# Three-part products added in one bank, attention by groups of four heads, and an order written out for three engines

## The chip, the cores and the metric

The kernel runs on one core of a Trainium2 chip. The metric is the device time of one execution in microseconds; less is better. The inputs are 64 batches of 256 rows by 512 columns, all in fp32, and the outputs are held to the fp32 reference.

## The reference, cut to what matters

```python
def gnn0(x, adj, Wq, bq, Wk, bk, Wv, bv, Wo, bo):     # 8 heads of 64
    q = (x @ Wq + bq).reshape(b, n, H, HD)             # k, v likewise
    scores = einsum('bqhd,bkhd->bhqk', q, k) / sqrt(HD)
    scores = scores + (1.0 - adj)[None, None] * -1e9
    out = einsum('bhqk,bkhd->bqhd', softmax(scores), v).reshape(b, n, d)
    return out @ Wo + bo

x = layernorm(x + gnn0(x, adj, ...))
y = einsum('nm,bmd->bnd', adj, x)
x = layernorm(x + einsum('bnd,do->bno', y, weight) + bias)
```

adj is 256 by 256 of zeros and ones, one eighth of them ones. There are five products with a 512 by 512 weight for each batch: q, k, v, o (the output of attention) and l (the second layer).

## The kernel before, in words

Two batches make a pair; there are NP = 32 pairs. `fast` does them all; `general` runs only where values leave the range that `fast` can treat (a small count at the end decides it), and it does not run here.

**Products in parts.** A large product is not done in whole fp32. Both operands are split into three fp32r parts (high, low, diff), and `part_product` (L318, its matmul is L321) multiplies part by part. A product is cut into four blocks j; a block is one PSUM bank of 128 by 512. `near` does parts 1 (low) and 0 (high) into the bank, then ACT multiplies the bank in place by 1 + 1/4096 (L333), and `far`, later, adds part 2 (diff) and takes the bank out: to R for o and l (L345, with the row sums for the norm), to V (L354), or to Q and K (L359). The two calls are held apart by a list, LAGGED, so that PE has other blocks between them. The split is `cut_low` (L168 masks bits off, L169 subtracts) and `difference` (L174) on DVE, and a rounding copy to high on ACT (L282 for x, L305 for o and l). Weights are split once (`split_w`), written to DRAM, and read again as parts for each pair through a ring of six 1 MB tiles (`load_w`, L127, on POOL's queue). Only v, q and k of the first two pairs take the weights as whole fp32.

**Attention.** A unit is four heads of one batch; a pair has four units. `scores` (L374) fills four banks, ACT takes the exponential (L378), DVE multiplies by the mask (L384) and adds the two halves of the keys (L390). `values` sums the exponentials with ones (L402, copied out at L404), multiplies by V (L410, copied at L413), and `divided` transposes, inverts and multiplies on DVE (L420 to L426).

**Norms and the second layer.** `norm` takes the mean from the row sums, ACT squares (L452), POOL takes the power -0.5 (L457), ACT applies scale and offset (L484). `halves` splits the result in two parts (L506 on ACT, L507 on DVE), `adj_x` multiplies by adj (L520) and ACT copies the bank to Y (L522), which `chunk_parts` then splits for l. `biased` (L436) adds a bias to R ahead of a product.

**Order.** A window w has scores and values of pair w, o and l of pair w - 1, v, q and k of pair w + 1, and x of pair w + 2. `between` writes the steps as a list, with four slots in which the values of the last unit and the scores of the next stand. Steps that follow on others are put off by a count of ticks (`later`). The list is the order of PE, ACT and DVE in windows 1 to 30; in window -1 of PE and DVE, in window 0 and in the last window of PE alone. Where an engine is not named, the framework's planner orders its instructions; SP's and POOL's queues are always its.

**Buffers.** PSUM has four banks for attention (`ps_at`) and four for the rest (`ps_mm`). A buffer is given out again when its last reader is done.

Of the kernel before, what the change touches and what calls it, by code (L numbers as in the profile page):

```python
# [19 lines left out]
FINE = 4096.0  # L32
MASKED = -1000000000.0
# [10 lines left out]
def fast(tc, x, adj, wq, bq, wk, bk, wv, bv, wo, bo, w1, b1, out):  # L44

    nc = tc.nc
# [6 lines left out]
    assert B % 2 == 0 and B > 2 and D == 512 and N == 256 and HD == 64  # L53
    qscale = 1.0 / math.sqrt(HD)

# [9 lines left out]
    xpool = pool("xp", 1)  # L65
    stage = pool("stage", 4)
    parts = pool("parts", 4)
    chunks = pool("chunks", 3)
    differences = pool("differences", 4)
    wring = pool("wr", 6)  # L70
    scratch = pool("scratch", 1, space=bass.MemoryType.DRAM)
    rpool = pool("rp", 2)
    one = pool("one", 1)
    qk = pool("qk", 3)
    four = pool("four", 4)
    small = pool("small", 2)
    ps_at = pool("ps_at", 4, space=bass.MemoryType.PSUM)
    ps_mm = pool("ps_mm", 4, space=bass.MemoryType.PSUM)

    XC, R, XF, XG, XL, XD, Q, K, V, E, SM, O, HL, Y, ST, CP, CUT = ({} for _ in range(17))  # L80

    def load_x(p, i):

        if p < NP:
            t = XC[p, i] = stage.tile([P, D], F32, name="x")
            for q in range(4):
                nc.sync.dma_start(t[q * 32:(q + 1) * 32].rearrange("i (m j) -> i m j", j=32), xb[p, i, q])

    def load_r(p):
        if p < NP:  # L90
            t = rpool.tile([P, 2, NC, D], F32, name="r")
            nc.sync.dma_start(t, xr[p])
            R[p] = [t[:, b] for b in range(2)]

    ones = cpool.tile([P, 32], F32, name="ones")
    nc.gpsimd.memset(ones, 1.0)
    for i in range(4):
        t = XC[0, i] = four.tile([P, D], F32, name="v")
        nc.sync.dma_start(t, xc[0, i // 2, i % 2])
    ident = one.tile([P, P], F32, name="zc")  # L100
    make_identity(nc, ident)
# [6 lines left out]
    def on_all(b, name):  # L108
# [5 lines left out]
    SOURCE = dict(v=wv, q=wq, k=wk, o=wo, l=w1)  # L114
    WP, SCRATCH, RAW = {}, {}, {}


    STREAM = [(name, p, i) for w in range(1, NP - 1) for name, p in
              (("o", w - 1), ("v", w + 1), ("q", w + 1), ("k", w + 1),
               *([("l", w - 1)] if w < NP - 2 else [("o", w), ("l", w - 1)])) for i in range(3)]  # L120

    def load_w(n=1):
        for _ in range(n):
            if STREAM:
                name, p, i = STREAM.pop(0)
                t = wring.tile([P, DC, D], F32R, name="wr")
                nc.gpsimd.dma_start(t, SCRATCH[name, i])  # L127
                WP[name, p, i] = t

    def raw_weight(name, tiles, queue):  # L130

        for i in range(3):
            SCRATCH[name, i] = scratch.tile([P, DC, D], F32, name=f"{name}{i}")
        n = DC // len(tiles)
        for i, t in enumerate(tiles):
            for k in range(n):
                RAW[name, i * n + k] = t[:, k]
            w = SOURCE[name][i * n * P:(i + 1) * n * P]
            if name == "o":


                for a in range(n):
                    queue.dma_start(t[:, a], w.rearrange("(h a i) e -> a h i e", h=4, a=2)[a])
            else:
                queue.dma_start(t, w.rearrange("(c p) e -> p c e", p=P))

    def split_w(name, k):

        high, low, diff = (parts.tile([P, D], F32R, name=n) for n in ("high", "low", "diff"))
        cut = one.tile([P, D], F32, name="cut")  # L150
        cut_low(RAW[name, k], cut, low)
        difference(RAW[name, k], low, diff)
        nc.scalar.activation(high, cut, AF.Copy)
        nc.scalar.activation(low, low.bitcast(F32), AF.Copy, scale=FINE)
        nc.scalar.activation(diff, diff.bitcast(F32), AF.Copy, scale=-1 / FINE)
        for i, part in enumerate((high, low, diff)):
            nc.sync.dma_start(SCRATCH[name, i][:, k], part.bitcast(F32))


    LOADS = [(1 + n // 4, n % 4) for n in range(4 * NP - 4)]  # L160

    def load_next():
        if LOADS:
            load_x(*LOADS.pop(0))

    def cut_low(a, cut, low):

        nc.vector.tensor_scalar(cut.bitcast(I32), a.bitcast(I32), -int(FINE), None, op0=OP.bitwise_and)  # L168
        nc.vector.tensor_tensor(low, a, cut, op=OP.subtract)  # L169

    def difference(a, low, diff):


        nc.vector.scalar_tensor_tensor(diff, low.bitcast(F32), -(FINE + 1), a, op0=OP.mult, op1=OP.add)  # L174

    raw_weight("v", [four.tile([P, 2, D], F32, name="o") for _ in range(2)], nc.scalar)

    nc.scalar.activation(small.tile([P, 1], F32, name="table"), ones[:, 0:1], AF.Exp)
    whole = lambda: [rpool.tile([P, DC, D], F32, name="r")]
    raw_weight("q", whole(), nc.sync)  # L180
    bq_s, bk_s = by_partition(bq, "bq"), by_partition(bk, "bk")
    raw_weight("k", whole(), nc.sync)
    adj_s = one.tile([P, NC, N], F32, name="sm")
    nc.sync.dma_start(adj_s, adj.rearrange("(c p) m -> p c m", p=P))
    for _ in range(4):
        load_next()
# [3 lines left out]
    bo_s, b1_s = on_all(bo, "bo"), on_all(b1, "b1")  # L190

    power = cpool.tile([P, 4], F32, name="power")
# [3 lines left out]
    acc = cpool.tile([P, N // 32], F32, name="acc")  # L196

    def adj_t():
# [6 lines left out]
        square = one.tile([P, NC, N], F32, name="vc")  # L205
# [3 lines left out]
        nc.vector.tensor_reduce(acc[:, 0:1], square, AX.XY, OP.max)  # L209
        nc.vector.tensor_scalar(acc, acc, RANGE * RANGE, None, op0=OP.mult)  # L210

    def bv_wo():

        wide = one.tile([P, DC, P], F32, name="vc")
        nc.vector.tensor_copy(wide, bv_s[:, :, None].to_broadcast([P, DC, P]))
        pm = ps_mm.tile([P, D], F32, name="mm")
        for d in range(DC):
            nc.tensor.matmul(pm, wide[:, d, :], RAW["o", d], start=d == 0, stop=d == DC - 1)
        nc.vector.tensor_tensor(bo_s, bo_s, pm, op=OP.add)
# [3 lines left out]
    due = []  # L223

    def later(n, f, *args):
        due.append([n, f, args])

    def tick():
        for d in due:
            d[0] -= 1  # L230
        ready = [d for d in due if d[0] <= 0]
        due[:] = [d for d in due if d[0] > 0]
        for _, f, args in ready:
            f(*args)

    BANKS = {}


    DEEP = [("l", NP - 3, 1), ("l", NP - 3, 3)] + [(n, p, j) for n in "ol" for p in (NP - 2, NP - 1) for j in (1, 3)]
    DEEP.remove(("o", NP - 2, 1))  # L240

    def x_t(p, i):
        xs = XC.pop((p, i))
        if p == 0:
            pt = ps_mm.tile([P, DC, P], F32, name="mm")
            if i == 0:
                for d in range(DC):
                    if d % 2 == 0:  # L250
                        t = qk.tile([P, 2, D], F32, name="kT")
                    XF[p, d] = t[:, d % 2]
            for d in range(DC):
                nc.tensor.transpose(pt[:, d, :], xs[:, d * P:(d + 1) * P], ident)
            for d in range(DC):
                to = XF[p, d][:, i * P:(i + 1) * P]
                if d % 2:
                    nc.scalar.activation(to, pt[:, d], AF.Copy)
                else:
                    nc.vector.tensor_copy(to, pt[:, d])  # L260
        else:
            if p > 1:
                XF[p, i] = xpool.tile([P, D], F32, name="xT")
                XC[p, i] = xs
            elif i % 2 == 0:
                t = four.tile([P, 2, D], F32, name="o")
                XF[p, i], XF[p, i + 1] = t[:, 0], t[:, 1]
            nc.vector.transpose(XF[p, i], xs)  # L268
            if p == 1:
                load_next()  # L270

    def x_parts(p, k):
        XG[p, k], XL[p, k] = (parts.tile([P, D], F32R, name=n) for n in ("high", "low"))
        cut_low(XF[p, k], XC[p, k], XL[p, k])
        later(1, x_high, p, k)

    def x_diff(p, k):
        XD[p, k] = parts.tile([P, D], F32R, name="diff")
        difference(XF.pop((p, k)), XL[p, k], XD[p, k])

    def x_high(p, k):
        nc.scalar.activation(XG[p, k], XC.pop((p, k)), AF.Copy)  # L282
        load_next()

    def chunk_parts(name, p, j):

        a = (O if name == "o" else Y)[p, j // 2][:, j % 2].rearrange("p k i -> p (k i)")  # L290
        cut = one.tile([P, D], F32, name="cut")
        if (name, p, j) in DEEP:
            high, low, diff = (parts.tile([P, D], F32R, name=n) for n in ("high", "low", "diff"))
        else:
            high, low = (chunks.tile([P, D], F32R, name=n) for n in ("chigh", "clow"))
            diff = differences.tile([P, D], F32R, name="cdiff")
# [27 lines left out]
    def near(name, p, j):  # L324
# [4 lines left out]
        if (name, p, 1) in WP:  # L329
            part_product(pm, name, p, j, 1)  # L330
# [510 lines left out]
```

## Time and profile before

| | us |
|---|---|
| median of 3 runs | 2533.59 (2533.59 to 2536.14) |
| span of the profiled execution, first to last instruction | 2536.9 |
| the profiled execution's own time | not listed apart from the span, which is 3.3 above the median |
| busy PE / DVE / ACT / POOL | 2492.1 / 1870.3 / 1709.9 / 386.1 |
| mean granted TensorE clock | 0.994 of full |
| moved by DMA | 600.25 MB, 237 GB/s in the mean |

A busy time is the union of an engine's instructions in the trace. Matmuls overlap, so PE's pace is read from the distances between starts in the timeline, not from its busy time or from a matmul's mean. In a line of the costliest groups come the source line, engine and operation, out<-in by the program's names, the shape and count, busy time and mean ns of one, and then the idle time ahead of them with what ended it.

### The profile page before, as it was taken

What the parts mean: (1) busy time and instruction counts of PE and PEld (TensorE: products, weight loads), DVE (VectorE), ACT (ScalarE), POOL (GpSimd) and SP (SyncE); (2) the same over time, 40 slices, a digit from 0 to 9 for tenths busy, and PEclk for the clock granted to TensorE, in tenths of its full rate; (3) what the DMA queues carried; (4) which work ended last, traced back from release to release, by engine and by line L of the source; (5) the groups of instructions that cost most, each with busy time, mean ns of one, the idle gap of its engine ahead of it and who ended that gap; (6) DMA issues with size and microseconds to landing.
All of it is one profiled execution on the core that took longest, in us unless ns stands there. A gap on an engine that the chain in (4) does not pass through costs nothing.

```text
span 2536.9 us, 42179 instructions
## 1 busy us (share of the span) xinstructions
PE 2492.1 (98%) x15806; PEld 1895.2 (75%) x15806; DVE 1870.3 (74%) x3239; ACT 1709.9 (67%) x3206; POOL 386.1 (15%) x793
## 2 busy tenths in 40 slices
PE   8999999999999999999999999999999999999997
PEld 4477777777777777777777777777777777777765
DVE  4577887777877768877768876778877778777687
ACT  4556666776666776667776667766667766667755
POOL 0111111111111111111111111111111111111111
PEclk9999999999999999999999999999999999999998
DMA  7777778687787787787787777877777877777721
GB/s 205 268 219 243 245 252 249 237 268 223 236 259 256 230 281 225 233 261 246 240 262 240 245 247 247 254 245 240 252 250 234 274 227 235 251 256 230 265 82 51
DMA packets 375744, 600.25 MB, mean 237 GB/s; under 512 B 273520, under 2 KB 273776, under 8 KB 317552
## 3 DMA queue, kind: packets, MB, share of 16 engines
q0 software_dynamic: 65232, 475.03, 52.0%
q1 hardware_dynamic: 309760, 121.42, 21.5%
q8 instruction: 127, 2.08, 0.3%
q10 hardware_dynamic: 544, 1.05, 0.1%
q14 instruction: 81, 0.66, 0.1%
HBM read 548.15 MB, written 49.28 MB: 235 GB/s over the span
## 4 chain that ended last, share of the span: by engine, by line
PE 68%; DVE 25%; issue 3%; DMA 1%; ACT 1%; POOL 0%; SPq 0%; DVEq 0%; ACTq 0%
PE mm L321 48%; PE at L374 7%; PE at L410 6%; PE mm L520 5%; DVE clow L169 4%; DVE cdiff L174 3%; DVE r L345 3%; DVE diff L174 3%; DVE cut L168 2%; PE at L402 2%; DVE low L169 2%; DVE xT L268 2%; DVE e L384 1%; DVE sm L390 1%; DVE x L168 1%
## 5 line engine op out<-in xcount | busy, mean ns | idle before, releaser
L333 ACT ACTIVATE mm<-mm 128x512 f32<-128x512 f32 x616 | 357.8, 581 | 349.4 <-PE mm L321 349.4
L384 DVE TENSOR_TENSOR e<-e,adjT 128x1024 f32<-128x1024 f32 x256 | 307.2, 1220 | 26.5 <-ACT e L378 26.5
L378 ACT ACTIVATE e<-at 128x512 f32<-128x512 f32 x512 | 265.2, 603 | 52.8 <-PE at L374 52.8
L321 PE MATMUL mm<-wr,clow 128*128 128x512 f32 x988 | 273.5, 399 | 9.7 <-DVE clow L169 5.6
L321 PE MATMUL mm<-wr,chigh 128*128 128x512 f32 x988 | 266.0, 391 | 0.0
L321 PE MATMUL mm<-low,wr 128*128 128x512 f32 x960 | 264.9, 398 | 0.0
L321 PE MATMUL mm<-wr,cdiff 128*128 128x512 f32 x988 | 260.6, 390 | 3.8 <-ACT mm L333 3.8
L374 PE MATMUL at<-qT,kT 64*128 64x256 f32 x2048 | 257.2, 389 | 0.8 <-ACT zc L404 0.7
L321 PE MATMUL mm<-high,wr 128*128 128x512 f32 x960 | 257.1, 390 | 0.0
L321 PE MATMUL mm<-diff,wr 128*128 128x512 f32 x960 | 248.4, 390 | 0.0
L410 PE MATMUL at<-e,v 128*32 128x256 f32 x4096 | 246.1, 379 | 0.0
L374 PEld LDWEIGHTS at<-qT,kT 64*128 64x128 f32 x2048 | 190.2, 186 | 69.4 <-issue 53.0
L507 DVE TENSOR_TENSOR hl<-r,hl 128x512 fp32r<-128x512 f32 x122 | 84.2, 691 | 203.3 <-ACT hl L506 203.3
L321 PEld LDWEIGHTS mm<-wr,clow 128*128 128x128 f32 x988 | 180.7, 188 | 68.7 <-DVE r L345 16.4
L452 ACT ACTIVATE z<-r,mean 128x512 bf16<-128x512 f32 x240 | 172.4, 719 | 78.8 <-DVE mean L444 75.0
L321 PEld LDWEIGHTS mm<-wr,cdiff 128*128 128x128 f32 x988 | 185.9, 188 | 43.7 <-ACT mm L333 4.6
L321 PEld LDWEIGHTS mm<-wr,chigh 128*128 128x128 f32 x988 | 186.2, 189 | 40.5 <-ACT chigh L305 0.8
L321 PEld LDWEIGHTS mm<-low,wr 128*128 128x128 f32 x960 | 173.5, 188 | 51.8 <-issue 19.9
L321 PEld LDWEIGHTS mm<-high,wr 128*128 128x128 f32 x960 | 180.2, 188 | 38.5
L345 DVE SCALAR_TENSOR_TENSOR r<-mm,r 128x512 f32<-128x512 f32 x240 | 162.5, 686 | 60.5 <-PE mm L321 60.5
L484 ACT ACTIVATE r<-r,less,rstd 128x512 f32<-128x512 f32 x248 | 200.0, 807 | 5.2 <-DVE less L477 5.2
L321 PEld LDWEIGHTS mm<-diff,wr 128*128 128x128 f32 x960 | 176.2, 188 | 33.7
(124 smaller groups left out, 4053.0 us busy)
## 6 DMA issues: line engine op xcount, KB each, us to landing
wr<-o POOLq DMA_DIRECT2D x93, 1024.0 KB, 6.0
wr<-v POOLq DMA_DIRECT2D x90, 1024.0 KB, 6.3
wr<-q POOLq DMA_DIRECT2D x90, 1024.0 KB, 6.5
wr<-k POOLq DMA_DIRECT2D x90, 1024.0 KB, 7.2
wr<-l POOLq DMA_DIRECT2D x90, 1024.0 KB, 7.7
x<-in_x_dram SPq DMA_DIRECT2D x496, 64.0 KB, 5.9
r<-in_x_dram SPq DMA_DIRECT2D x31, 1024.0 KB, 5.4
out_dram<-r SPq DMA_DIRECT2D x60, 512.0 KB, 6.5
```

The lines of the kernel that those rows point to most:

```text
L169: nc.vector.tensor_tensor(low, a, cut, op=OP.subtract)
L174: nc.vector.scalar_tensor_tensor(diff, low.bitcast(F32), -(FINE + 1), a, op0=OP.mult, op1=OP.add)
L321: nc.tensor.matmul(pm, *operands(name, p, j, i, k), start=k == 0 and i == begins, stop=k == DC - 1, skip_group_check=True)
L333: nc.scalar.activation(pm, pm, AF.Copy, scale=1 + 1 / FINE)
L345: nc.vector.scalar_tensor_tensor(r, pm, 1.0, r, op0=OP.mult, op1=OP.add, accum_out=ST[p, name][:, j:j + 1])
L374: nc.tensor.matmul(sc[s][:, a, :], K[p, g][r, a, b, kc * P:(kc + 1) * P], Q[p, g][r, a, b, :], start=True, stop=True)
L378: nc.scalar.activation(e[:, s], sc[s], AF.Exp, scale=qscale)
L384: nc.vector.tensor_tensor(e, e, mask[:, kc:kc + 1, :].to_broadcast([P, 4, N]), op=OP.mult)
L410: nc.tensor.matmul(at[h * 32:(h + 1) * 32, a, :], V[p, b][:, kc, col:col + 32], e[kc][:, h % 2, h // 2, :], start=kc == 0, stop=kc == NC - 1)
L452: nc.scalar.activation(waste, R[p][j // 2][:, j % 2], AF.Square, bias=mean[:, j:j + 1], accum_out=squares[:, j:j + 1])
L484: nc.scalar.activation(r, r, AF.Identity, scale=rstd, bias=less)
L520: nc.tensor.matmul(pm[:, j, :], hl[:, i, mc, j * P:(j + 1) * P], adjT[:, mc, :], start=mc == 0 and i == 0, stop=mc == NC - 1 and i == 1)
```

## The change

The parts are taken another way. ACT makes high from a scaled copy (scale 4096/4095 times a little less than one); low is the rest after high times 4095/4096; diff is made of high and low alone. The factor between the parts is then the same for all three products, so all twelve matmuls of a block follow each other into one bank, and the factor 4095/4096 is applied when the bank is taken out. The bit mask, the scaling of the bank in between, LAGGED and the put-off steps go. The Y copy goes too: high and the rest are taken from adj_x's bank.

A unit of attention is now four heads of both batches: two a pair. PSUM is divided into five and three banks. The norm works by batch (two columns) and no longer by pair (four). q and k are done by group of heads: the first group of pair w + 1 during pair w, the second in its own turn. Only q and k of the first group of pair 0 are whole fp32. Weights come in stages of three 1 MB tiles, in a ring of two stages; the stage after next is asked for when one ends. The order is written out in `start`, `first`, `second` and `last`, and it holds for PE, ACT and DVE in `first` and `second`, for PE alone in `start` and `last`.

```diff
-    ps_at = pool("ps_at", 4, space=bass.MemoryType.PSUM)
-    ps_mm = pool("ps_mm", 4, space=bass.MemoryType.PSUM)
+    ps_at = pool("ps_at", 5, space=bass.MemoryType.PSUM)
+    ps_mm = pool("ps_mm", 3, space=bass.MemoryType.PSUM)
...
+    def end_stage():
+        ended[0] += 1
+        if ended[0] + 1 < len(STAGES) and ended[0] > 1:
+            load_w(STAGES[ended[0] + 1])
...
+    def rest(parts, a):
+        high, low, diff = parts
+        nc.vector.scalar_tensor_tensor(low, high.bitcast(F32), -RHO, a, op0=OP.mult, op1=OP.add)
+        nc.vector.scalar_tensor_tensor(diff, low.bitcast(F32), -FINE, high.bitcast(F32), op0=OP.mult, op1=OP.add)
...
+    def product(name, p, j):
+        pm = ps_mm.tile([P, D], F32, name="mm")
+        pairs = [operands(name, p, j, k) for k in range(DC)]
+        n = len(pairs[0])
+        for i in range(n):
+            for k in range(DC):
+                nc.tensor.matmul(pm, *pairs[k][i], start=i == 0 and k == 0, stop=i == n - 1 and k == DC - 1)
+        scale = RHO if n == 3 else 1.0
...
+    def adj_x(p, b, half):
...
+            set_high("l", p, b, half, pm)
+            rest(SET["l", p, b, half], pm)
...
+    def first(w):
+        q, n = w - 1, w + 1
+        values(q, 1, [(squared, q - 1, "l", 2), (squared, q - 1, "l", 3)])
+        scores(w, 0)
+        do((inverse, q - 1, "l", 1), masks(w, 0, 0),
+           (o_high, q, 0, 1), (o_high, q, 1, 1), (block, "v", w, 0), (o_rest, q, 0, 1), (o_rest, q, 1, 1),
+           (less, q - 1, "l", 1), masks(w, 0, 1),
+           (block, "v", w, 1), (normed, q - 1, "l", 2), (normed, q - 1, "l", 3),
+           (with_bo, q, 0), (with_bo, q, 1),
+           (block, "v", w, 2), (x_t, n, 0), (block, "v", w, 3), (x_t, n, 1), (stage_end, w),
+           (block, "q", w, 2), (block, "k", w, 2), (block, "q", w, 3), (block, "k", w, 3), (stage_end, w),
+           (x_high, n, 0), (x_high, n, 1),
+           (block, "o", q, 0), (x_rest, n, 0), (x_t, n, 2), (x_high, n, 2),
+           (block, "o", q, 1), (mean, q, "o", 0), (squared, q, "o", 0), (squared, q, "o", 1),
+           (x_rest, n, 1), (x_t, n, 3), (inverse, q, "o", 0), (x_high, n, 3),
+           (block, "o", q, 2), (x_rest, n, 2), (less, q, "o", 0), (normed, q, "o", 0), (normed, q, "o", 1),
+           (block, "o", q, 3), (mean, q, "o", 1), (x_rest, n, 3), (hl_high, q, 0, 0), (hl_high, q, 0, 1), (stage_end, q))
+
+    def second(w):
+        q, n = w - 1, w + 1
+        values(w, 0, [(squared, q, "o", 2), (squared, q, "o", 3), (hl_low, q, 0, 0), (hl_low, q, 0, 1)])
+        scores(w, 1)
+        do((inverse, q, "o", 1), (with_b1, q, 0),
+           (block, "q", n, 0), (less, q, "o", 1), (normed, q, "o", 2), (normed, q, "o", 3),
+           (adj_x, q, 0, 0), masks(w, 1, 0),
+           (block, "k", n, 0), (hl_high, q, 1, 0), (hl_high, q, 1, 1), (hl_low, q, 1, 0), (hl_low, q, 1, 1),
+           (adj_x, q, 0, 1), masks(w, 1, 1)[:1],
+           (block, "q", n, 1), (with_b1, q, 1),
+           (adj_x, q, 1, 0), (block, "k", n, 1), (stage_end, n), (adj_x, q, 1, 1), masks(w, 1, 1)[1:],
+           (block, "l", q, 0), (block, "l", q, 1), (mean, q, "l", 0), (squared, q, "l", 0), (squared, q, "l", 1),
+           (o_high, w, 0, 0), (inverse, q, "l", 0), (o_rest, w, 0, 0),
+           (block, "l", q, 2), (less, q, "l", 0), (normed, q, "l", 0), (normed, q, "l", 1),
+           (block, "l", q, 3), (mean, q, "l", 1), (o_high, w, 1, 0), (o_rest, w, 1, 0), (stage_end, q))
...
+    with tc.manual_schedule(engines={PE}):
+        start()
+    with tc.manual_schedule(engines={PE, DVE, ACT}):
+        for w in range(1, NP):
+            first(w)
+            if w < NP - 1:
+                second(w)
+    with tc.manual_schedule(engines={PE}):
+        last()
```

`values` takes the steps in its second argument between its two copies on ACT: zc, those steps, vc of both batches. `normed` of l stores the rows and asks for R of pair p + 2; `x_t` of row k asks for row k of the next pair. `start` does x, then q and k of the first group in whole fp32, the splits of all weights between the blocks of pair 0, and q and k of the first group of pair 1. `last` does what is left after `first(31)`: scores and values of the second group of pair 31, o of pair 31, and l of pairs 30 and 31.

## The prediction

> **What bounds the kernel now.** I began with the page: its busy shares, its forty slices and its costliest groups.
>
> ```profile
> span 2536.9 us, 42179 instructions
> PE 2492.1 (98%) x15806; PEld 1895.2 (75%) x15806; DVE 1870.3 (74%) x3239; ACT 1709.9 (67%) x3206; POOL 386.1 (15%) x793
> PE   8999999999999999999999999999999999999997
> ...
> L333 ACT ACTIVATE mm<-mm 128x512 f32<-128x512 f32 x616 | 357.8, 581 | 349.4 <-PE mm L321 349.4
> ```
>
> TensorE is busy in every slice but the first and last; DVE and ACT have a quarter and a third of the span free. The costliest ACT group is the scaling in the bank, which the change removes, but ACT waits for PE there (349.4 us), not PE for it. Does PE ever wait? PE's list of waits (total, times, longest):
>
> ```profile
> PE mm L321 <- DVE clow L169: 5.6, 3, 3.2
> ...
> PE mm L321 <- ACT mm L333: 4.7, 3, 2.1
> PE mm L321 <- DVE low L169: 3.6, 3, 2.2
> PE at L402 <- DVE sm L390: 3.3, 19, 0.5
> PE mm L321 <- DVE o L268: 2.3, 1, 2.3
> ```
>
> The list sums to about 30 us, nearly all of it before 150 us or after 2440 us. In the middle only the 19 waits for the sum of the exponentials recur. Since a busy PE need not be PE at its peak, I read how far apart groups start, in PE's timeline, once where the weights are whole fp32 and then in one steady window:
>
> ```profile
> 24.89 13.90 PE L321 MATMUL mm<-kT,r 128*128 128x512 f32 x32
> 38.62 0.60 PE L202 MATMUL mm<-zc,sm 128*128 128x128 f32 x4
> ...
> 854.51 0.64 PE L402 MATMUL at<-sm,ones 128*32 128x256 f32 x8
> 854.97 1.91 PE L410 MATMUL at<-e,v 128*32 128x256 f32 x32
> 856.81 2.00 PE L374 MATMUL at<-qT,kT 64*128 64x256 f32 x16
> 858.73 1.20 PE L321 MATMUL mm<-low,wr 128*128 128x512 f32 x4
> 859.77 1.07 PE L321 MATMUL mm<-high,wr 128*128 128x512 f32 x4
> 860.68 1.07 PE L321 MATMUL mm<-wr,diff 128*128 128x512 f32 x4
> ...
> 931.30 0.64 PE L402 MATMUL at<-sm,ones 128*32 128x256 f32 x8
> ```
>
> The same place comes back after 931.30 - 854.51 = **76.79 us**: one pair of batches. Four part matmuls take 0.907 us (859.77 to 860.68 is 0.91), a block of twelve 2.72; one attention unit 0.46 + 1.84 + 1.92 = 4.22; an adj_x 0.945 (two: 1.89). A pair needs 20 blocks (54.4), 4 units (16.9) and 4 adj_x (3.8): 75.1 us. So a steady pair loses only 1.7 us. Sixteen whole-fp32 matmuls, half of one v, q or k, are two records each: 13.8 us for 16, against 10.9 for the same product in parts.
>
> [...] I walk the new order queue by queue. [...]
>
> **The change, part by part.** *PE's steady work does not change.* A pair still has 240 part matmuls, the same scores, values, sums and adj_x. Joining two batches halves the moves from scores into a block, each 0.13 us slow (858.73 to 859.77 is 1.03, not 0.907): -0.26 us a pair.
>
> *Removed from ACT and DVE.* The scaling at L333 (20 a pair at 0.581: 11.6 us of ACT), the Y copy at L522 (4 x 0.598 = 2.4 us), the cuts at L168 (12 x 0.42 = 5.1 us of DVE). Halving z, reciprocal and rs saves DVE 1.0 us; six more small norm operations at 0.165 cost 1.0. ACT goes from about 53 to 39 us a pair, DVE from 58 to 53. All this lies beside PE; its direct gain is the 4.7 us of the list above and I count none.
>
> *The first two pairs.* Before, six products of 16 matmuls are whole fp32 (v, q, k of pairs 0 and 1); afterwards only q and k of the first group of pair 0, one product's worth. Five times 13.8 - 10.9: **-15 us**. Walk of the new start: first product at about 9.5 us as now (the same rows and about as many bytes land first), raw q and k 13.8 (the first block now takes 1.6 more; kept), adjacency 0.5, scores 4.0, v 10.9, q and k 10.9, values and scores 8.6, bv_wo 3.5, pair 1's q and k 10.9: 74. DVE has 20 splits and 8 x parts at 1.34, masks 13.7 and some 15 us more in it, 66 us, so it runs nearly full; I add 4 us (0 to 12): 78. The waits of the old start (2.3 at 55 us, 3.2 + 0.6 at 123, 3.6 around 143, slow clock after them) mostly have no place in it.
>
> *The new order.* I use the distance of starts in the steady window: ACT 0.50 for a copy or exp, 0.52 a high, 0.60 q/k, 0.70 normed, 0.86 squared; DVE 0.61, a dependent pair 1.34, masked or summed 1.14; PE to ACT or DVE 0.2, between those 0.05; the power on POOL with both hand-overs about 1.1.
> - first(w), PE: 4.60 values + 3.84 scores + 0.13 + 12 blocks = 41.2. At its end DVE adds o1, ACT squares twice, POOL, two normed, two hl_high: ACT is free 2.4 us after PE has gone on, DVE also.
> - second(w): behind that backlog ACT copies zc, squares twice and copies vc0, done at 5.3; the second scores want vc0's bank at 5.56. The last two of the eight want banks at 7.48 that the second and third exp free at 6.9 and 7.46. So five banks just suffice, with 0.0 to 0.2 us in hand. In the next first(w) the backlog is 2.1, the same outcome.
> - later in second(w): normed o2 and o3 stand behind q0 on ACT, adj_x's high behind them (14.1), its two DVE steps, then three mask operations, then hl_low: 19.6. PE wants it at 18.6: **1.1 us wait**. The next k block wants the adj_x bank that DVE must now read (a bank used to be freed by the Y copy): 0.3.
> - so a pair takes 41.2 + 35.5 = 76.7, against 76.8. Removing steps and joining units gains what the late hl_low takes. I add 0.3 for waits too small for such a walk (0 to 1).
>
> *Queues and DMA.* Weights stay 15 MB a pair, and x, r and out stay too; SP's loads keep their kinds and follow x_t. The tight load is o's: requested as v ends (17.6 to 19.5 into first), needed at 30.3. [...] I take 0; with r, out and two rows of x in its way up to 2.4 us a pair.
>
> *The end.* last() has 53.3 us of PE work; the norm chain ahead of the last adj_x and the parts after them leave about 5.5 of waits, and the tail after the last product is 10 (now 2527.8 to 2536.9, 9.1).
>
> **Sum:** 78 + 31 x 41.2 + 30 x 35.5 + 69 = 2489, and 30 x 0.3: **2498** as a span, 39 below 2536.9. The page's execution spans 3.3 more than the median of 2533.59, so the median becomes **2495**.
>
> **The rivals.**
> 1. *ACT falls behind on the attention banks (slower).* All norms hang on a power in POOL's queue, which also holds the weight loads, waiting for PE:
>
> ```profile
> POOL wr L127 <- PE mm L321: 1282.5, 444, 9.3
> ```
>
> If the scheduler puts l's load ahead of the power of o0, that power waits until o3 ends, 1.6 us later; the same for the load after l3, 0.8. With no slack in the five banks this goes to PE: 2.4 us a pair, 72 in all: 2567. It decides from 39 / 30 = 1.3 us a pair. For it: no slack, and a strict order on ACT and DVE. Against it: in the steady window now the power always runs before the load that follows.
> 2. *Fewer waits.* If hl_low comes before the masks in time, 1.7 a pair fall away: about 2445 to 2465. Against it: the order is fixed, and the chain is eight steps long.
> 3. *o's weights come late:* up to 2.4 a pair, again near 2565. For it: DMA is at 77% already. Against: no wait of PE for weights anywhere now.
> 4. *The start gains nothing,* since DVE's 66 us bind it, and the steady pair is 0.5 worse: about 2530, no change.
>
> **How the numbers follow.** The main case, 2480 to 2518: 0.50; rival 2: 0.15; rival 1 (2530 to 2600): 0.22; rival 3: 0.08, with 0.03 of it still below the old time; rival 4: 0.05. About 0.2%, 5 us, is what a measurement can tell from no change: faster 0.68, same 0.05, slower 0.27. The range of 2455 to 2575 leaves out the better part of rival 2 and the worse of 1 and 3; the main case alone is 2480 to 2518.
>
> **What would show it.** PE's period should be 76 to 77.5 us, with one recurring wait of about 1 us for hl's second half ahead of adj_x and one of 0.3 ahead of the k block; no L333; ACT near 39 and DVE near 53 us a pair; PE leaving the start at 74 to 82 us. A period over 78.1, with scores waiting for ACT's exps or vc, means rival 1; matmuls waiting for DMA mean rival 3; under 76, rival 2.

## The result, and the profile after

| | before | after |
|---|---|---|
| median, us | 2534.18 (2533.31 to 2536.14, 7 runs) | 2527.16 (2526.39 to 2527.86, 7 runs) |
| ratio, 95% interval | | 0.9971 (0.9961 to 0.9982) |
| span of the profiled execution, us | 2536.9 | 2525.6 |
| busy PE / DVE / ACT, us | 2492.1 / 1870.3 / 1709.9 | 2445.6 / 1685.6 / 1299.9 |

The kernel is faster by 7 us, where 39 were forecast. The head of the page first:

```profile
span 2525.6 us, 39920 instructions
PE 2445.6 (97%) x15886; PEld 1937.2 (77%) x15886; DVE 1685.6 (67%) x2807; ACT 1299.9 (51%) x2418; POOL 443.7 (18%) x726
PE   7599999999999999999999999999999999999997
```

410 us of ACT's work and 185 of DVE's are gone, and the old L333 (the scaling in the bank) with them, and the span is only 11 shorter. By the medians it is 7: in the runs on record a span is about 1.8 us shorter than the run's time (2525.6 and 2527.36 for this profile), so the old page, with a span of 2536.9, shows an execution some 4.5 us above its median. The first two slices, 63 us each, show 7 and 5 where the old page had 8 and 9. PE's list of waits (total, times, longest) says what for:

```profile
PE mm L304 <- ACT v L315: 24.1, 1, 24.1
PE mm L460 <- DVE hl L450: 20.4, 30, 0.7
PE mm L233 <- ACT e L237: 8.3, 1, 8.3
...
PE mm L304 <- DVE low L254: 4.2, 3, 1.8
PE mm L304 <- DVE sl L254: 3.9, 2, 2.8
PE mm L220 <- DVE z L217: 1.5, 1, 1.5
```

One wait recurs, 30 times 0.68 us: hl's second half ahead of adj_x. Two single waits, 8.3 and 24.1 us, are new. In PE's timeline the sums L333 open each `first` and `second`:

```profile
841.32 1.07 PE L333 MATMUL at<-sm,ones 128*32 128x256 f32 x16
876.63 1.07 PE L333 MATMUL at<-sm,ones 128*32 128x256 f32 x16
917.80 1.07 PE L333 MATMUL at<-sm,ones 128*32 128x256 f32 x16
```

A `second` is 876.63 - 841.32 = 35.31 us, the next `first` 41.17, a pair 76.48. Laid beside the sum of the prediction, with the same lines at 85.08, 153.12 and 2447.16 as bounds:

| stage | predicted | measured | off by |
|---|---|---|---|
| start | 78 | 85.1 | +7.1 |
| `first` of pair 1 | 41.2 | 68.0 | +26.8 |
| 30 steady pairs | 30 x 77.0 | 30 x 76.47 | -16.0 |
| `last` and tail | 69 | 78.4 | +9.4 |

The four sum to +27.3, the span's 2525.6 against 2498 but for rounding. The steady stage came out as walked, and its 0.2 us below the walk and the unused allowance of 0.3 a pair make up the -16.0. What is missing went at the two ends.

**The 8.3 us wait.** ACT's timeline from 8 us on (start, duration, instruction, idle before):

```profile
11.77 1.30 ACT L124 ACTIVATE wr<-sh 128x512 fp32r<-128x512 f32 x2 [8.48 <-DMA sh<-in_L_gnn_Wv_dram]
14.53 1.30 ACT L124 ACTIVATE wr<-sh 128x512 fp32r<-128x512 f32 x2 [1.47 <-DMA sh<-in_L_gnn_Wv_dram]
15.74 0.26 ACT L237 ACTIVATE e<-mm 128x128 f32<-128x128 f32 x1
```

`start` fixes the order of PE alone. The planner put four splits of v, which wait for v's weights to land, ahead of the first copy of transposed x (L237), for which PE was waiting. The first product starts at 18.96 us, not 9.5.

**The 24.1 us wait.** PE, ACT, DVE and SP's queue around it, a fence each:

```profile
125.93 2.07 PE L304 MATMUL mm<-wr,low 128*128 128x512 f32 x4 [24.09 <-ACT v L315]
```

```profile
103.33 0.63 ACT L127 ACTIVATE sh<-sh 128x512 fp32r<-128x512 f32 x1 [5.39 <-DVE sh L126]
...
125.29 1.56 ACT L315 ACTIVATE v<-mm 128x512 f32<-128x512 f32 x3
```

```profile
102.61 0.69 DVE L126 SCALAR_TENSOR_TENSOR sh<-sh 128x512 fp32r<-128x512 f32 x1 [3.94 <-DMA o<-sh]
```

```profile
64.08 18.77 SPq L80 DMA_DIRECT2D x<-in_x_dram  x8
82.89 1.97 SPq L134 DMA_DIRECT2D o<-sh  x4
```

Read backwards: three product banks are full and PE waits for V's copies; these stand in ACT's queue behind the rest of eight splits of o's and l's weights and four copies for o's left operand (L268), which take the same `sh` tiles; a split needs three of four `sh` tiles and so waits until its forerunner's parts have landed in DRAM; and the first such write left SP only at 82.89 us, behind eight loads of x. In the trace no copy of V overtakes a waiting split: PE stops at 101.8 us with its banks full, ACT is idle for up to 5.39 us at a time, and the copies of V run only at 125.29, behind the last of that work. That every queue keeps strict order, as the prediction's walk has it, was its author's assumption.

### The profile page after: what moved, and what is told of

Its sections match the earlier page's. It is cut to its first block, busy times and chain, and to the rows that moved or that the text cites. A ratio compares the mean times of both kernels' runs of the same rounds, so it can differ in the third digit from the quotient of the medians.

```text
span 2525.6 us, 39920 instructions
## 1 busy us (share of the span) xinstructions
PE 2445.6 (97%) x15886; PEld 1937.2 (77%) x15886; DVE 1685.6 (67%) x2807; ACT 1299.9 (51%) x2418; POOL 443.7 (18%) x726
## 5 line engine op out<-in xcount | busy, mean ns | idle before, releaser
L416 ACT ACTIVATE waste<-r,mean 128x512 bf16<-128x512 f32 x256 | 184.3, 720 | 220.4 <-DVE mean L409 216.3
L304 PE MATMUL mm<-wr,sl 128*128 128x512 f32 x1008 | 274.7, 394 | 3.9 <-DVE sl L254 3.9
L304 PE MATMUL mm<-wr,sh 128*128 128x512 f32 x1008 | 270.9, 390 | 0.0
L304 PE MATMUL mm<-wr,sd 128*128 128x512 f32 x1008 | 270.5, 390 | 0.0
L304 PE MATMUL mm<-diff,wr 128*128 128x512 f32 x1008 | 269.7, 389 | 0.0
L422 POOL TENSOR_TENSOR rstd<-squares,power 128x2 f32<-128x2 f32 x128 | 149.2, 1166 | 670.8 <-DVE squares L421 539.7
L304 PEld LDWEIGHTS mm<-wr,sh 128*128 128x128 f32 x1008 | 189.8, 188 | 40.1
L304 PEld LDWEIGHTS mm<-wr,sl 128*128 128x128 f32 x1008 | 187.4, 189 | 43.1 <-DVE sl L254 4.9
L304 PEld LDWEIGHTS mm<-wr,sd 128*128 128x128 f32 x1008 | 189.8, 188 | 39.6
L320 ACT ACTIVATE qT<-mm,bq 128x512 f32<-128x512 f32 x128 | 88.0, 688 | 242.5 <-PE mm L304 242.5
```

Source lines behind the costliest of these rows:

```text
L304: nc.tensor.matmul(pm, *pairs[k][i], start=i == 0 and k == 0, stop=i == n - 1 and k == DC - 1)
L320: nc.scalar.activation(T[p, b][:, c].rearrange("p b i -> p (b i)"), pm, AF.Identity, bias=bias[:, j:j + 1], scale=scale)
L416: nc.scalar.activation(waste, R[p][b][:, c], AF.Square, bias=t[0][:, c:c + 1], accum_out=t[1][:, c:c + 1])
L422: nc.gpsimd.tensor_tensor(t[2], t[1], power, op=OP.pow)
```

## The experiments

Each time is a median with its range; ratios are to the kernel before, measured beside it.

**e1: writes of o's and l's parts from GpSimd's queue.**

```diff
-        nc.sync.dma_start(to, part.bitcast(F32))
+        queue.dma_start(to, part.bitcast(F32))
...
-            keep(name, i, k, t[i])
+            keep(name, i, k, t[i], nc.gpsimd)
```

> The changed kernel with one edit: the parts of o's and l's weights are written to DRAM from POOL's queue and no longer from SP's, where the trace shows the first of them issued at 82.9 us behind sixteen loads of x. Theory A (the 24.1 us wait of PE at 101.7 us comes of SP's order: the splits can only go on as these writes land, and first(1)'s V copies stand behind the splits in ACT's queue): the splits run from 45 us on, the wait goes, with it 2.5 us of slow clock: 2497 to 2504 us against 2527. Rival B (the ring of four tiles alone sets the pace, about 3.2 us a split, wherever the writes are issued from): the wait moves ahead into the start or stays, and at most 8 us are gained: 2519 to 2530. Rival C (POOL's queue now holds v's reload up): PE waits for the weights of v in first(1), 2520 or more.

Measured: 2521.3 (2520.8 to 2521.5), 0.9948 (0.9934 to 0.9961). The 24 us wait is gone, and `first` takes 45.2 us; but the splits, free to go from 45 us on, now stand in the start, which ends at 102.4 instead of 85.1. They still wait for each other's landing, as DVE's timeline shows:

```profile
53.94 0.69 DVE L126 SCALAR_TENSOR_TENSOR sh<-sh 128x512 fp32r<-128x512 f32 x1 [4.80 <-DMA o<-sh]
```

The time is that of rival B. So SP's queue set where the wait fell; that the ring of four tiles makes the splits wait is seen in the landing waits that are left.

**e2: x's copies in written order, alone.** The four `x_first` steps were moved under an order of PE, DVE and ACT of their own.

> The changed kernel with one edit: the four x_first steps of the start are in written order on ACT and DVE too, so that the splits of v's weight, which wait for that weight to land at 11.8 us, cannot stand ahead of the copies of the transposed x. Theory A (PE's wait of 8.3 us at 9 us is ACT's and DVE's queues blocked by those splits): the first product starts at about 10.5 instead of 19.0 us. If the 24 us wait behind it is paced by the splits' writes, which do not move with PE, part of the gain is taken back there: 2519 us if it is kept, 2527 if it is wholly eaten by the later wait. Rival B (the first product would have waited for its weights or the last rows anyway): it starts at 15 us or later.

Measured: 2527.2 (2525.4 to 2528.0), 0.9972, with the wait of 8.31 us still there. The edit missed its aim: an order binds only the steps written into it, and the splits of v, outside, still stood ahead of L237. It says nothing on the theory; e8 does.

**e3: hl_low ahead of the sum of the first batch's exponentials,** and with_b1 of the second batch behind the third adj_x.

```diff
-           (adj_x, q, 0, 0), masks(w, 1, 0),
+           (adj_x, q, 0, 0), masks(w, 1, 0)[:2],
...
-           (adj_x, q, 0, 1), masks(w, 1, 1)[:1],
-           (block, "q", n, 1), (with_b1, q, 1),
-           (adj_x, q, 1, 0), (block, "k", n, 1), ...
+           (adj_x, q, 0, 1), masks(w, 1, 0)[2:], masks(w, 1, 1)[:1],
+           (block, "q", n, 1),
+           (adj_x, q, 1, 0), (with_b1, q, 1), (block, "k", n, 1), ...
```

> The changed kernel with one edit in second(w): on DVE the two hl_low of the second batch come ahead of the sum of the first mask group, and with_b1 of the second batch comes after the parts of the third adj_x. Theory A (the wait of 0.68 us in each steady pair is DVE's order, and nothing else is late right behind it): the period falls from 76.48 to 75.8 us, 30 pairs give 20 us: about 2507 us. Rival B (the next thing is late at once: the adj_x bank for the first block of l, which became free within 0.1 us of its use): the period falls by 0.1 at most, 2524 to 2527 us.

Measured: 2501.6 (2501.3 to 2502.0), 0.9869 (0.9854 to 0.9885): 25.6 us faster than the change. PE's timeline:

```profile
833.79 1.07 PE L333 MATMUL at<-sm,ones 128*32 128x256 f32 x16
868.25 1.07 PE L333 MATMUL at<-sm,ones 128*32 128x256 f32 x16
```

`second` is 34.46 us instead of 35.31, `first` 41.17 as before, and hl is no longer in the list of waits. The 0.85 us a pair is more than the 0.68 that the list showed. The change's timeline has the rest:

```profile
859.93 0.28 PE L460 MATMUL mm<-adjT,hl 128*128 128x256 f32 x1
860.89 1.10 PE L460 MATMUL mm<-adjT,hl 128*128 128x256 f32 x7 [0.68 <-DVE hl L450]
```

The second matmul of this adj_x starts 0.96 us after the first, where 0.12 is the usual distance (eight in 0.945): 0.84 lost. The list counts only the idle time behind the first one's record of 0.28.

**e4: ACT's work put back.** Twenty copies without use a pair. ACT's busy time in a pair goes from 39.84 to 49.85 us, 10.0 more.

```diff
+            if 0 < p < NP - 1:
+                idle = one.tile([P, D], mybir.dt.bfloat16, name="waste")
+                nc.scalar.activation(idle, b1_s, AF.Copy)
```

> The changed kernel with work put back on ACT: after each of the 20 blocks of pairs 1 to 30 ACT copies 128 by 512 constants into a waste tile, about 12 us of ACT a pair, as much as the scaling in the bank that the change removed. Its output does not depend on it. Theory A (ACT's removed work lay beside PE; ACT is at 39.8 of 76.5 us): no more than 5 us longer, 2527 to 2532 us. Rival B (the chains through ACT at the end of first and second have nothing in hand, so each copy ahead of zc or of the exps goes to PE): 0.5 to 1 us a pair, 2542 to 2557 us.

Measured: 2545.4 (2543.9 to 2546.2), 1.0043 (1.0030 to 1.0057): 18 us slower than the change, 0.61 a pair. Its list of waits:

```profile
PE mm L460 <- DVE hl L450: 35.4, 30, 1.2
```

The attention banks hardly stalled: the scores of a `second` take 3.99 us instead of 3.92. PE waits longer at the place where it already waited, for hl's second half; which copy in the chain of norm, halves and hl_low delays it was not traced.

**e5: a second set of tiles for every other split** (two tiles of `hl`).

> Every second split of o's and l's weights goes into two tiles of the pool hl instead of three of the four tiles sh, so that two splits can be under way while their parts are written. Theory A (the ring of four sh tiles, freed only when a part has landed in DRAM, paces the eight splits and so holds up the V copies behind them on ACT): from the first write at about 83 us the splits go in pairs of 3.2 us, done near 97 instead of 125; PE's 24.1 us wait at 102 to 126 shrinks below 5, time about 2527 - 20 = 2507 (2502 to 2514). Theory B (SP issues the writes late and slowly, so a second set only lets one more split go ahead): the wait stays above 15 us, time 2519 to 2527. Nothing changes in the steady pair (76.5 us) under either.

Measured: 2518.5 (2518.2 to 2519.4), 0.9942 (0.9929 to 0.9956). The wait for V falls from 24.1 to 16.0 us, as theory B has it (above 15), and the time lies half a microsecond below that theory's range. The last of ACT's idle times ahead of V's copies is now 5.20 us, for a tile of o's left operand that waits for a part of l to land.

**e7: four banks for attention and four for products.**

> Attention gets four PSUM banks instead of five, the products four instead of three; nothing else. Theory A (five banks just suffice, as the prediction's walk has it): scores now wait for ACT's exps in each of the two attention units of a pair, 0.5 to 1.5 us a pair, time 2540 to 2570. Theory B (the exps run ahead of the need with slack, and three product banks are what is tight): the time stays at 2520 to 2530. The wait of PE for hl's second half (0.68 us a pair) stays in both.

Measured: 2564.3 (2563.1 to 2565.2), 1.0123 (1.0108 to 1.0139). Scores of one unit, in the change and here:

```profile
881.08 3.92 PE L375 MATMUL at<-qT,kT 64*128 64x256 f32 x32
```

```profile
861.73 4.41 PE L375 MATMUL at<-qT,kT 64*128 64x256 f32 x32
```

Both units of a pair take about 0.5 longer; a pair takes 77.41 us, 28 of the 37 us over 30 pairs. The fifth bank is needed, as theory A has it.

**e8: the start up to adj's transposes in written order on three engines.**

> The steps of the start up to the adjacency's transposes are bound in the written order on PE, DVE and ACT instead of on PE alone: x's transposed copies, then the whole fp32 q and k products with one split of v behind each. Theory A (the 8.3 us wait at 9 to 17.4 us comes only from ACT's order, four v splits that wait for wv ahead of x's copies): the first product starts near 10 us instead of 17.4, the start ends at 77 to 79 instead of 85.1 and the time falls by 6 to 8, to about 2520. Theory B (the start is paced by DVE, some 66 us of splits, masks and parts in it, so what PE gains at 10 us it loses again before 85): the first product is earlier by 7, the start ends at 83 or later, the time is 2524 to 2528.

Measured: 2527.0 (2525.5 to 2528.2), 0.9974 (0.9964 to 0.9984), no gain. PE's timeline:

```profile
10.65 16.20 PE L304 MATMUL mm<-e,r 128*128 128x512 f32 x32 [0.48 <-issue]
31.34 5.33 PE L375 MATMUL at<-qT,kT 64*128 64x256 f32 x28 [3.42 <-ACT kT L320]
69.69 5.40 PE L220 MATMUL mm<-sl,z 128*128 128x512 f32 x8 [2.70 <-DVE z L217]
85.94 1.07 PE L333 MATMUL at<-sm,ones 128*32 128x256 f32 x16
```

The first product starts 8.3 us earlier and the start ends 0.9 later. K's copy stands behind a split (3.42), bo's product waits longer (2.70 for 1.48), and after each wait the matmuls run slow: 5.33 us for 28 of the 32 records of scores (3.92 for all 32 in the change), 5.40 for bo's four whole fp32 matmuls (two records each) that took 3.70. DVE is busy 9.9 of the 10 us from 20 to 30. These are the second theory's numbers, but its reason is shown only in part, for just before that stretch DVE stood idle:

```profile
17.56 0.71 DVE L244 STREAM_TRANSPOSE xT<-x 128x512 f32<-128x512 f32 x1 [6.38 <-DMA x<-in_x_dram]
```

A transpose for pair 1, outside the written order, was put ahead of v's splits and waited for its row to land; on ACT the first split stands behind q's first copy, at 17.17. DVE's first split so runs at 18.20, where it ran at 12.43 in the change. In the whole start DVE is busy 50.6 of 85.9 us. What fills it from 18 to 30 us is work that was put off; 66 us of it are not in this stage. v's splits ahead of q's first copy, and that transpose behind them, were not tried.

**e9: l's splits between the blocks of the first `first`,** with e5's tiles. The first of the four stands ahead of v's third block, the others behind the fourth.

> l's four splits, and the parts of o's left operand that need their tiles, move from the end of the start into the first first(w), behind its v blocks; every second split has its own tiles as in the two-sets run. Theory A (V copies wait on ACT behind the splits of o and l): with only o's four splits ahead the 24.1 us wait falls below 4, the first first(w) takes 43 to 48 us instead of 68, time 2503 to 2509. Theory B (the wait only moves: the l splits now hold up the q and k copies in the same stage while their parts land, 3.2 us each): the first first(w) still takes 54 us or more and the time is 2514 to 2522. Theory C (o's splits alone are late enough): the V copies still wait 10 us or more.

Measured: 2528.7 (2524.2 to 2530.4), 0.9976 (0.9968 to 0.9984); `first` still takes 67.9 us. PE's waits:

```profile
PE mm L308 <- DVE sl L258: 17.1, 4, 12.4
...
PE mm L308 <- ACT v L319: 8.3, 1, 8.3
```

PE waits 8.3 us for V's copies, of which the last two stand in ACT's queue behind l's first split, and then 12.4 for o's parts, behind the later ones. The wait moved, as theory B has it, though the time is longer than its 2514 to 2522. As one split still stood ahead of half of V, theory A was not tested cleanly.

**e10 and e11: the mended parts together.** Both have e1, e3, e5 and e8. In e10 the whole start has a written order on three engines, with the splits spread between the blocks; in e11 the later start is left to the planner.

> Four edits at once: hl_low ahead of the second pair of masks (as in the hl_low run), parts of o and l written from GpSimd's queue, two sets of tiles for their splits, and the whole start in the written order on PE, DVE and ACT, with the eight splits spread one by one between the blocks from about 45 us on. Theory A (the waits of the start come from the order of ACT and DVE and from SP's queue, and go when both are given): 25.6 us from the steady pairs, as measured alone, and 15 to 25 from start and first first(w), which end together at 128 to 138 us instead of 153: 2478 to 2487. Theory B (the start is full: DVE's work, the transfers and ACT bind it whatever the order, so what one wait gives back another takes): the first first(w) ends at 142 us or later and the time is 2490 to 2502.

> The same but for the start behind the adjacency's transposes, whose order on DVE and ACT is left to the planner, as in the changed kernel. Theory A (the order matters more than the queue and the tiles): the planner puts splits in the way of what PE needs again, first first(w) ends at 140 to 147 us, 6 to 15 us behind the written order, time 2488 to 2496. Theory B (with queue and tiles mended the order is indifferent): within 3 us of the written order.

Measured: e10 2497.0 (2494.8 to 2498.8), 0.9855 (0.9840 to 0.9870); e11 **2481.6** (2480.0 to 2482.9), **0.9796 (0.9782 to 0.9809)**, the best version. e10 came out as its theory B has it (the first `first` ends at 150.3). For e11 neither theory holds: the planner's order is 15 us faster than the written one, in which PE waits 9.94 us for K's copy. In e11 the sums that open `first` and `second` (L337 there):

```profile
91.99 1.07 PE L337 MATMUL at<-sm,ones 128*32 128x256 f32 x16
133.56 1.07 PE L337 MATMUL at<-sm,ones 128*32 128x256 f32 x16
```

The first `first` takes 41.57 us: the 41.2 of the walk, once V's copies no longer have to wait. Start and `first` end at 133.6 instead of 153.1; of the span's 47.1 us that is 19.6, and 30 times 0.90 a pair (75.57 measured) is 27.

**e12: K's second copy ahead of the last two splits of v,** on e11.

> The kernel with the planned order of the late start (e11), in which the second whole fp32 k product's copy on ACT is placed ahead of the last two splits of v instead of between them. Theory A (the 4.4 us wait of PE for kT at 27 to 31 us, and the slow clock behind it, come from ACT's order alone): the scores follow the products without a wait, and the time falls by 4 to 6.5 us, to 2475 to 2478. Theory B (DVE, which is full from 17 to 45 us, binds the start): what the scores gain, the v block loses in waiting for its x parts; the second group of sums still starts within 1.5 us of 59.2, and the time is within 2 us of 2481.6.

Measured: 2487.4 (2486.4 to 2488.5), 0.9815 (0.9801 to 0.9828): slower than e11 by 6. The scores wait 1.15 + 1.29 us instead of 4.36, the v block then 1.09 and 0.53 for x's low parts, and the next sums stand at 60.04 against 59.19. Up to there it is the second theory: DVE is busy 12.4 of the 13 us from 18 to 31, again after an idle time (7.17 us) for a row of pair 1. The time is not within that theory's 2 us. The start then ends at 93.9 (92.0) and `first` takes 45.4, with a wait for K's copy in it (1.86) and slow matmuls behind (5.51 us for 28 records of scores, a clock of 0.83 from 100 to 110); the planner's order of the rest is another than in e11, and no run takes that apart.

## Why the prediction was wrong, point by point

- **What bounds, and the steady pair: right.** First 41.2 against 41.17, second 35.5 against 35.31, one recurring wait at hl's second half (1.1 forecast, 0.68 measured, 0.85 recovered by e3). The second wait, 0.3 ahead of the k block, did not show. That `second` agrees so well is in part luck: the walk has 34.1 without waits and 1.4 of waits, e3 shows 34.46 without the wait and 0.85 for it. ACT was forecast near 39 and DVE near 53 us a pair; the window 841.32 to 917.80 has 39.84 and 51.85. The 0.3 a pair for small waits, 9 us, was not used.
- **Five banks just suffice: right as far as it was tested.** With five no wait for exps recurs, with four each unit loses 0.5 (e7). How little is in hand was not measured.
- **"All this lies beside PE ... I count none": wrong of the new order.** Put back there, 10.0 us of ACT's work cost 0.61 a pair (e4), at the wait for hl. The sum was not hurt, since the wait was walked in the new order without that work. What the scaling cost in the old order no run tells.
- **The failed step: the start.** The sentence was "DVE ... runs nearly full; I add 4 us (0 to 12): 78", and behind it a plain 41.2 for the first `first`. The total of PE's work held, the 15 us for fewer whole fp32 products included: without the waits of 8.29 and 1.48 and the slow half microsecond (four part matmuls in 1.34 us instead of 0.907, at 73.65), 85.1 is 75. And DVE did not run full: it was busy 50.2 of the 85.1 us, since seven of the eight splits of o and l did not get done there. What failed is that DVE's work was added up and taken for the bound, while ACT's and SP's queues were not walked in a stage whose order only PE had. The splits of o and l counted as 1.34 us of DVE each; they cost their landing too, 6.5 to 3.2 us from one to the next once SP had let the writes go, and they stood ahead of V: 24.1 us and 2.7 of slow clock behind it (0.50 from 125.93 to 131). e1 and e5 show that neither the queue nor the tiles alone is the cause: the one edit moved the wait, the other left 16.0 of it; e9 moved the place of four splits and the wait with them. e11, with queue, tiles and the early order mended at once, took 19.6 of the 34 us that the two stages were over. Whether all three are needed was not tried.
- **Rival 4, the start gains nothing because DVE binds it (2530), was nearest in time,** and at most half right in mechanism. DVE is full from about 18 to 30 us in e8 and e12, but idle for 6 to 7 us before that, and its 66 us were 50; the larger loss, around 102 to 126, was no lack of DVE but the wait for landing. Its steady pair, 0.5 worse, was wrong.
- **Rivals 1 and 3: neither occurred.** The list has one wait for exps, 0.5 us, in `last`, and none for weights by DMA. In the `first` that opens at 876.63 us, o's three loads of 1 MB, asked for at 894.60 to 896.41, took 5.3 to 8.8 us to land, ahead of the first block of o at 906.83; in the old kernel such a load took 5.0 us at best and 6.9 in the median. The prediction's 0, and its 2.4 us a pair for late weights, were its author's estimates. Rival 2's mechanism came true only when the order was changed (e3), and gave 25.6 us, 0.85 of the 1.7 a pair that it had.
- **`last`: 69 forecast, 78.4 measured.** The waits were 8.5 and not 5.5, the tail 11.1 and not 10. PE's work took 58.8 and not 53.3: about 3 of the 5.5 are matmuls at half pace (a clock of 0.52) between 2463.7 and 2469.6, behind two waits, and 0.9 is in scores that took 4.8 instead of 3.85; the rest is spread in small pieces. The sum had no such term. No run tried to mend it.
- **From span to median: the wrong way.** The prediction took off 3.3 us, as the old page's span lies above the old median. Here the median is 1.6 above the span. So the median is 32 us off, where the span is 27.6.

## What to carry to other kernels

Where the order of only one engine is fixed, walk the queues of the others instruction by instruction, with each buffer's release by DMA as a step of its own; a sum of busy time per engine hides a copy that stands behind a waiting one. A stage that runs once can lose as much as 30 steady periods give, so it deserves the same walk. And when a wait has several causes in series, mending one can move it, as e1 and e9 did: mend them together before judging any.

## What the hardware showed

**TensorE came back slow behind some waits.** The windows below hold the stretch behind the wait for V, a steady pair, and a stretch of `last`; the third last column is the granted clock.

```profile
125.90:136.00 10.10, 10.07 (x33) 8.11 (x34) 8.94 (x10) 2.24 (x4) 1.63 (x3) 0.73 0.65 232
841.32:917.80 76.48, 75.80 (x497) 60.35 (x497) 51.85 (x86) 39.84 (x75) 14.23 (x23) 1.00 0.75 248
2462.00:2472.00 10.00, 8.93 (x29) 6.84 (x30) 6.12 (x10) 0.00 (x0) 0.00 (x0) 0.66 0.01 2
```

In the last, groups of four part matmuls start 1.71 us apart instead of 0.907 (2464.70 to 2466.41), 1.9 times as far, and the clock from 2463.7 to 2469.6 is 0.52. PE counts as busy for 8.93 of those 10 us: a busy PE is not PE at its pace here. Records of matmuls overlap, too: in a steady pair those of four part matmuls last 1.07 us and start 0.907 apart.

The waits ahead were 24.09 us for V, 2.82 and 1.07 with two matmuls between in `last`, and 2.70 alone in e8, with a clock of 0.84 from 70 to 80 us, where the ten us before and after have 0.99 and 1.00. In e11, behind 4.36 us, it is 0.71 from 31 to 41. The old kernel's start has 0.51 from 57.15 to 60.00, behind 2.26 us, 0.62 from 125.80 to 129.88, behind 3.19, and 0.50 from 147.42 to 151.43, behind 0.77 and 2.16. Not every wait was followed by a lower clock: 1.83 us in `last` was not (1.00 from 2480.8 to 2485), nor 8.29 in the start (1.00 from 17.4 to 34.3, though the 32 records of whole fp32 products take 15.50 us there and 13.90 in the old kernel from 24.89 on). What sets the two kinds apart was not shown. The two waits of e8 cost 1.7 to 1.9 us more behind them, the one for V 2.7, the two in `last` about 3.

**Loads and writes in one queue.** In e1 the writes of o's and l's parts leave the queue of x's loads, for one that loads weights, and the time falls by 6 us. A full separation was not tried. Of SP's loads of x, 64 KB each, the first sixteen took 10.36 us, 0.65 each; the eight at 64.08 took 18.77, 2.3 each in the mean. What makes the later ones slow was not tried.
